# Ending the banks of a GNN aggregate one by one, and moving transposed rows by DMA instead of by TensorE

## The chip, the cores and the metric

The kernel runs on one core of one Trainium2 chip. The metric is the device time of one execution in microseconds (us); lower is better.

## The reference

Two graph layers over 2708 nodes with 1024 features, float32. Each normalises x, forms a score for every pair of nodes, masks it with the adjacency matrix, takes a softmax over the neighbours and adds the weighted mean of the transformed nodes to x.

```python
# layer 0
f = x @ Wf + bf;  g = x @ Wg + bg
scores = where(adj > 0, relu(f @ g.T), NEG)
x_new = softmax(scores, axis=1) @ (x @ W + bW)
# layer 1
h = input @ W
scores = where(adj > 0, leaky_relu(h @ a1 + (h @ a2).T, 0.2), NEG)
x_new = relu(softmax(scores, axis=1) @ h)
# both: h = max(layernorm(x), 0);  x = x + layer(h, adj, ...)
```

## The kernel before

The nodes of the output are cut into five panels of 576, 576, 532, 512 and 512. For each panel and layer there is a *score* stage (layer 0 only), an *aggregate* (softmax weights times features) and a *project* stage (times W). Products use seven half-size products M1 to M7 in place of eight, in the order M1, M5, M2, M6, M3, M7, M4. Each sums in a group of four PSUM banks, and two groups are alive at a time: M6 and M7 (gz) take the banks that M2 (gx) leaves, and what follows M3 takes those that M3 (gy) leaves.

The order of products inside one M, and where its banks are emptied:

```python
            for k, d in ([(k, d) for k in range(K) for d in range(NH)] if by_k else
                         [(k, d) for d in range(NH) for k in range(K)]):
                nc.tensor.matmul(ps[d], left(m, k, d), right(m, k), start=(start and k == 0),
                                 stop=(k == K - 1 and m not in more), skip_group_check=True)
                ...
            if by_k:
                if m in more:
                    more[m](ps)            # the leftover products of all four banks
                for d in range(NH):
                    evict[m](d, ps[d])     # then all four evictions
```

In the middle of M7 the leftover products of M1 and M5 go through four more banks, gw, and VectorE adds them into m15 (the profile calls that tile m):

```python
        def into_m15():
            ps = [bank(f"gw{d}")[:, :h] for d in range(NH)]
            left_over(ps, 1, hi, True)
            for d in range(NH):
                add(get("m15", d), ps[d], get("m15", d))
```

M4's group, gv, takes the banks that gw leaves free. A vector that lies as columns is put on all partitions by TensorE transposes with a broadcast operand:

```python
    def spread(o, cols):
        at = 0
        for g in range(0, len(cols), 4):
            ps = bank("sp_ps")
            ...
                nc.tensor.transpose(ps[:, w:w + n], cl.to_broadcast([n, P]), ident[:n, :n])
            copy(o[:, at:at + w], ps[:, :w])
```

It is used for r (one vector per panel, needed by the score stage as rb) and for two vectors of scores, z and c (the profile calls c "none"), needed by layer 1's weights as ub and vb. While layer 1 aggregates panel p it makes the weights of panel p+1: after M3 the columns (`take_shifts`), after M7 the weights themselves (`take_weights`):

```python
    def take_shifts(p):
        flush()
        got["zm"] = shifts1(p)
    ...
        # one unit of the weights
        nc.scalar.activation(s, vb1[:n, :w], AF.Identity, bias=f2s[:n, t:t + 1])
        nc.vector.scalar_tensor_tensor(s, ub[:n, :w], f[1][:n, t:t + 1], s, op0=OP.add, op1=OP.max)
        add(s, s, mk[0][:n, :w])
        nc.scalar.activation(s, s, AF.Exp)
```

The order of the calls is not the order of the instructions: a scheduler orders each engine's queue at build time, except where the program asks for program order.

## Time and profile before

| | before |
|---|---|
| median, first 3 runs | 3149.56 us (3143.49 to 3149.83) |
| profiled span | 3144.7 us |
| TensorE busy | 3053.0 us, 97% |
| granted TensorE clock, mean | 0.990 |

In the views PE is TensorE (PEld its weight loads), DVE VectorE, ACT ScalarE, POOL GpSimd and SP SyncE; a q behind the name marks the engine's sequencer, which issues DMAs. *Landing* is the time from the issue of a transfer to the semaphore that tells of its end.

The order of time on VectorE and ScalarE around M7 of layer 1's first aggregate (columns: start, length, engine, line, operation, output<-inputs, records, and in brackets the idle time of the engine before it and what ended it):

```profile
2283.87 1.55 DVE L45 TENSOR_TENSOR m<-gw,m 128x288 f32<-128x288 f32 x4 [4.92 <-PE gw L816]
...
2296.14 2.10 ACT L45 ACTIVATE P<-vb,f2s 128x576 f32<-128x576 f32 x3
2296.95 1.55 DVE L45 SCALAR_TENSOR_TENSOR P<-ub,f,P 128x576 f32<-128x576 f32 x2 [2.35 <-ACT P L45]
```

The four adds that empty gw come at 2283.87, 9.3 us ahead of gv's first product at 2293.15. The new weights (P) start 12 us later.

### The profile page before, as it was taken

The page shows a single profiled execution, that of the slowest core. Times are in us where ns is not written, and L with a number is a line of the kernel's source. Part 1 is how long each engine was busy: PE and PEld are TensorE (multiplying, and loading weights), DVE is VectorE, ACT ScalarE, POOL GpSimd, SP SyncE. Part 2 cuts the span into 40 slices and gives each one's busy share as a digit, 9 for nine tenths or more (in the row PEclk, how much of TensorE's full clock was granted, in tenths as well). Part 3 has the DMA queues.
Part 4 walks back from the last instruction along what each step waited for, and adds up shares of the span by engine and source line. Part 5 has one row for each costly group of instructions (what it writes and reads, how often), then busy time and mean ns, then how long its engine had stood idle before and what let it go on. Part 6 is the DMA issues. An engine that isn't in the chain of part 4 may idle for free.

```text
span 3144.7 us, 36222 instructions
## 1 busy us (share of the span) xinstructions
PE 3053.0 (97%) x12712; PEld 2263.8 (72%) x12712; DVE 1827.6 (58%) x3730; ACT 447.0 (14%) x788; POOL 462.8 (15%) x664
## 2 busy tenths in 40 slices
PE   8988999999999999999999999997999999999998
PEld 4566777667877588876888885865757758678684
DVE  5867686286732687327881478658573471745612
ACT  3321020000200102001020002103031130211200
POOL 2643002210002100023000101020010020120102
PEclk9989999999999999999999999998999999999999
DMA  6888938878446796478945677686655565565655
GB/s 215 308 285 270 263 124 310 231 228 252 148 129 168 217 263 200 143 177 245 294 157 153 174 214 235 215 285 209 205 178 174 156 203 156 170 195 172 214 161 192
DMA packets 379045, 651.82 MB, mean 207 GB/s; under 512 B 170784, under 2 KB 211264, under 8 KB 378864
## 3 DMA queue, kind: packets, MB, share of 16 engines
q1 hardware_dynamic: 335920, 525.38, 55.7%
q0 software_dynamic: 42944, 124.13, 11.8%
q8 instruction: 101, 1.65, 0.2%
q14 instruction: 80, 0.66, 0.1%
HBM read 536.68 MB, written 112.67 MB: 206 GB/s over the span
## 4 chain that ended last, share of the span: by engine, by line
PE 83%; DMA 5%; issue 4%; DVE 4%; POOL 2%; SPq 1%; ACT 0%; POOLq 0%; DVEq 0%; ACTq 0%
PE gz L551 12%; PE gy L551 12%; PE gx L551 11%; PE sz L1061 7%; PE gv L551 5%; PE pz L953 5%; PE sy L1061 4%; PE sx L1061 4%; PE px L953 4%; PE py L953 4%; PE qz L551 3%; PE qy L551 2%; PE qx L551 2%; PE M_ps L467 2%; SPq L139 1%
## 5 line engine op out<-in xcount | busy, mean ns | idle before, releaser
L1061 PE MATMUL sz<-B,As 128*128 128x288 f32 (+2 forms) x1200 | 292.7, 393 | 8.2 <-DVE st L45 7.5
L1061 PEld LDWEIGHTS sz<-B,As 128*128 128x128 f32 x1200 | 227.7, 190 | 58.2 <-DVE st L45 11.9
L857 POOL TENSOR_TENSOR gT<-gT,rr 128x2304 f32<-128x2304 f32 (+5 forms) x20 | 72.7, 3635 | 1102.0 <-DVE rr L45 999.3
L1061 PE MATMUL sx<-B,As 128*128 128x288 f32 (+2 forms) x800 | 201.6, 395 | 13.2 <-DMA As<-hs_d 12.2
L1061 PE MATMUL sy<-B,As 128*128 128x288 f32 (+2 forms) x800 | 199.0, 392 | 0.0
L551 PE MATMUL gz<-P,hc 128*128 128x288 f32 (+2 forms) x800 | 186.0, 393 | 2.3 <-ACT gT L45 2.3
L551 PE MATMUL gz<-Sa,hc 128*128 128x288 f32 (+2 forms) x800 | 186.0, 393 | 2.3 <-ACT gT L45 2.3
L551 PE MATMUL gx<-P,hc 128*128 128x288 f32 (+2 forms) x800 | 186.1, 394 | 0.0
L1061 PEld LDWEIGHTS sx<-B,As 128*128 128x128 f32 x800 | 152.3, 191 | 45.4 <-DMA As<-hs_d 13.1
L551 PE MATMUL gy<-T,hc 128*128 128x288 f32 (+2 forms) x800 | 184.2, 391 | 0.0
L551 PEld LDWEIGHTS gz<-Sa,hc 128*128 128x128 f32 x800 | 151.2, 190 | 36.0 <-ACT gT L45 4.4
L551 PEld LDWEIGHTS gx<-P,hc 128*128 128x128 f32 x800 | 153.1, 192 | 32.8 <-issue 1.9
L551 PEld LDWEIGHTS gz<-P,hc 128*128 128x128 f32 x800 | 150.9, 190 | 35.6 <-ACT gT L45 4.4
L551 PEld LDWEIGHTS gy<-T,hc 128*128 128x128 f32 x800 | 152.0, 190 | 30.5
L1061 PEld LDWEIGHTS sy<-B,As 128*128 128x128 f32 x800 | 151.7, 190 | 30.6 <-DVE st L45 0.3
L953 PE MATMUL py<-w,ps 128*128 128x512 f32 x320 | 143.1, 597 | 4.7 <-DMA w<-in_L_gnn_W_dram 4.7
L953 PE MATMUL pz<-w,ps 128*128 128x512 f32 x320 | 142.8, 597 | 0.8 <-DVE pt L45 0.8
L953 PE MATMUL px<-w,gT 128*128 128x512 f32 x320 | 141.9, 596 | 0.7 <-issue 0.7
L143 POOL DMA_DIRECT2D out_dram<-x_res x180 | 88.9, 501 | 265.3 <-DVE x_res L45 259.0
L45 DVE TENSOR_TENSOR gT<-gy,u 128x288 f32<-128x288 f32 (+2 forms) x40 | 14.8, 431 | 183.5 <-PE gy L816 183.5
L953 PEld LDWEIGHTS py<-w,ps 128*128 128x128 f32 x320 | 60.5, 191 | 81.1 <-issue 77.5
L45 DVE TENSOR_TENSOR u<-gz,m 128x288 f32<-128x288 f32 (+2 forms) x40 | 17.6, 439 | 171.1 <-PE gz L551 170.7
(318 smaller groups left out, 5063.6 us busy)
## 6 DMA issues: line engine op xcount, KB each, us to landing
hc<-hg_d SPq DMA_DIRECT2D x350, 512.0 KB, 3.9
As<-hs_d SPq DMA_DIRECT2D x150, 512.0 KB, 5.8
w<-wt_d SPq DMA_DIRECT2D x96, 512.0 KB, 5.1
w<-in_L_gnn_W_dram SPq DMA_DIRECT2D x72, 512.0 KB, 4.3
md<-md_d SPq DMA_DIRECT2D x56, 512.0 KB, 4.6
adj_i<-in_adj_dram SPq DMA_DIRECT2D x200, 128.0 KB, 5.0
hg_d<-g POOLq DMA_DIRECT2D x40, 512.0 KB, 4.9
hs_d<-hsT POOLq DMA_DIRECT2D x40, 512.0 KB, 5.3
```

The source lines that it names most:

```text
L45: i = f(*a, **k)
L139: tc.keep_in_program_order(nc.sync.dma_start(a, b))
L143: nc.gpsimd.dma_start(a, b)
L467: nc.tensor.matmul(ps, wfT[a][c // NH][:, c % NH, :], wgT[b][c], start=(c == 0), stop=(c == NC - 1))
L551: nc.tensor.matmul(ps[d], left(m, k, d), right(m, k), start=(start and k == 0), stop=(k == K - 1 and m not in more), skip_group_check=True)
L857: nc.gpsimd.tensor_tensor(of(e, s), of(e, s), by(s, k), OP.mult)
L953: nc.tensor.matmul(ps, left[i][m][:, k, :], w_[k], start=(start and k == 0), stop=(k == NH - 1), skip_group_check=True)
L1061: nc.tensor.matmul(ps[:n, :h], lefts[q][:, i % 2, c, :n], B[m][c // 2][:, c % 2, :h], start=(start and c == 0), stop=(c == NH - 1), skip_g ...
```

## The change

The intent is threefold: let each bank of an M end on its own, so that its eviction runs beside the next bank's products; take r's spreads off TensorE for panels 1 to 4; and take layer 1's two score spreads off TensorE for panels 1 to 4. Each of these vectors goes to HBM as a row of 4-byte elements and comes back broadcast to all partitions. The cut below leaves out the stop flags and the calls of `behind` (which runs queued softmax work between products); these move with the loops.

```diff
+    def columns_to_row(row, p, col):
+        k = len(pieces[p])
+        nc.gpsimd.dma_start(row[0:1, :W].rearrange("o (i p) -> p (o i)", p=P), col[:, :F])
+        if k > F:
+            n = pieces[p][F][1]
+            nc.gpsimd.dma_start(row[0:1, W:W + n].rearrange("o n -> n o"), col[:n, F:k])
+    def row_on_all(o, row, p):
+        load(o[:, :width[p]], row[0:1, :width[p]].to_broadcast([P, width[p]]))
@@ accumulate
-            for k, d in ([(k, d) for k in range(K) for d in range(NH)] if by_k else
-                         [(k, d) for d in range(NH) for k in range(K)]):
+            whole = K - TAIL                                   # TAIL = 2
+            for k, d in ([(k, d) for k in range(whole) for d in range(NH)] + [(k, d) for d in range(NH) for k in range(whole, K)]
+                         if by_k else [(k, d) for d in range(NH) for k in range(K)]):
...
+                if by_k and d == NH - 1 and k == whole - 1 and m in more:
+                    more[m](ps)
+                if k == K - 1:
                     evict[m](d, ps[d])
...
-                for d in range(NH):
-                    evict[m](d, ps[d])
@@ score stage
-        spread(rb, columns_of(p, r_[:, first_col[p]:]))
+        if p == 0:
+            spread(rb, columns_of(p, r_[:, first_col[p]:]))
+        else:
+            row_on_all(rb, r_d[p], p)
@@ after layer 0's first aggregate
+            for s in range(1, NP):
+                columns_to_row(r_d[s], s, r_[:, first_col[s]:])
@@ weights1
+            if p > 0:
+                for o, row in zip((ub, vb1), uv_d[p]):
+                    row_on_all(o, row, p)
+                return
@@ take_shifts
+        for row, col in zip(uv_d[p], got["zm"]):
+            columns_to_row(row, p, col)
```

More of the change, by code (lines that the diff above doesn't have):

```diff
@@ L162 @@
     mk_d = [dram.tile([P, NQ + 1, 2, width[p]], BF, name=f"mk_d{p}") for p in range(NP)]
+    r_d = [dram.tile([1, WX], FP, name=f"r_d{p}") for p in range(NP)]
+    uv_d = [[dram.tile([1, WX], FP, name=f"uv{k}_d{p}") for k in range(2)] for p in range(NP)]
     x1_d = [dram.tile([P if t < TINY else NY, D], FP, name=f"x1_d{t}") for t in range(NT)]
@@ L535 @@
         picks.append(t)
+    TAIL = 2
     def accumulate(left, right, K, h, order, then, evict, name, prepare={}, rate=0.0, by_k=False, more={}, room=()):
@@ L548, in accumulate @@
             ps = [t[:, :h] for t in acc[at[m]]]
-            for k, d in ([(k, d) for k in range(K) for d in range(NH)] if by_k else
-                         [(k, d) for d in range(NH) for k in range(K)]):
-                nc.tensor.matmul(ps[d], left(m, k, d), right(m, k), start=(start and k == 0),
-                                 stop=(k == K - 1 and m not in more), skip_group_check=True)
-                if by_k and d == NH - 1 and k % 3 == 2:
+            whole = K - TAIL
+            for k, d in ([(k, d) for k in range(whole) for d in range(NH)] + [(k, d) for d in range(NH) for k in range(whole, K)]
+                         if by_k else [(k, d) for d in range(NH) for k in range(K)]):
+                nc.tensor.matmul(ps[d], left(m, k, d), right(m, k), start=(start and k == 0), stop=(k == K - 1),
+                                 skip_group_check=True)
+                if by_k and d == NH - 1 and k < whole and (k % 3 == 2 or k == whole - 1):
                     behind(rate)
@@ L556, in accumulate @@
                     more[m, k]()
-                if not by_k and k == K - 1:
+                if by_k and d == NH - 1 and k == whole - 1 and m in more:
+                    more[m](ps)
+                if k == K - 1:
                     evict[m](d, ps[d])
-                    behind(rate, m in room)
+                    if not by_k:
+                        behind(rate, m in room)
             if by_k:
-                if m in more:
-                    more[m](ps)
-                for d in range(NH):
-                    evict[m](d, ps[d])
                 behind(rate)
@@ L815, in left_over @@
                 g = slice(B32 * d, B32 * d + NY)
-                nc.tensor.matmul(ps[d], two[g, W:], S[TINY][g, s], start=False, stop=True, skip_group_check=True)
+                nc.tensor.matmul(ps[d], two[g, W:], S[TINY][g, s], start=False, stop=start, skip_group_check=True)
         def into_m15():
```

## The prediction

> **What bounds the kernel now.** I read the page first: busy time per engine, the forty slices, the chain that ended last.
>
> ```profile
> span 3144.7 us, 36222 instructions
> PE 3053.0 (97%) x12712; PEld 2263.8 (72%) x12712; DVE 1827.6 (58%) x3730; ACT 447.0 (14%) x788; POOL 462.8 (15%) x664
> PEclk9989999999999999999999999998999999999999
> PE 83%; DMA 5%; issue 4%; DVE 4%; POOL 2%; SPq 1%; ACT 0%; POOLq 0%; DVEq 0%; ACTq 0%
> ```
>
> TensorE is busy 97% of the span at nearly full clock and carries 83% of the chain. So only two things can shorten the program: fewer TensorE cycles, or fewer of the 3144.7 - 3053.0 = 91.7 us in which it stands still. No matrix product goes away, so already here the change is small.
>
> Second, TensorE's waits, totalled by releaser (columns: us in total, times, longest).
>
> ```profile
> PE sx L1061 <- DMA As<-hs_d: 12.2, 2, 12.0
> PE mx_ps L740 <- DVE mx L45: 9.9, 1, 9.9
> PE qx L551 <- ACT m L45: 9.7, 1, 9.7
> PE sum_ps L755 <- DVE gT L45: 5.1, 10, 0.5
> PE gz L551 <- ACT gT L45: 4.5, 10, 0.5
> PE sp_ps L237 <- DVE m L45: 3.0, 1, 3.0
> ```
>
> The change addresses the two rows with count 10, one wait per aggregate (5 panels x 2 layers): M6's banks (gz) wait for M2's eviction to gT, and the row sums (sum_ps) wait for M3's. The long single waits belong to the first panel and the layer boundary; the diff leaves them.
>
> Third, TensorE in order of time at the end of M3 and M7 in layer 1's first aggregate (columns: start, length, line, tiles, records, idle before).
>
> ```profile
> 2264.45 2.10 PE L812 MATMUL gy<-P,hl 128*128 128x288 f32 x8
> 2266.49 0.77 PE L816 MATMUL gy<-P,hl 20*128 20x288 f32 x8
> 2267.79 1.24 PE L755 MATMUL sum_ps<-sm,ones 128*128 128x288 f32 x4 [0.53 <-DVE gT L45]
> ...
> 2283.78 8.03 PE L551 MATMUL gz<-P,hc 128*128 128x288 f32 x32
> 2291.64 0.80 PE L237 MATMUL sp_ps<-ident,z 128*128 128x128 f32 x5
> 2292.37 0.85 PE L237 MATMUL sp_ps<-ident,none 128*128 128x128 f32 x5
> 2293.15 3.18 PE L551 MATMUL gv<-P,hc 128*128 128x288 f32 x12
> ```
>
> The leftover products (hl) end all four banks almost together, then TensorE stands for one eviction. At M7's end, 2293.15 - 2291.64 = 1.51 us go to ten transposes that spread two columns.
>
> **What the Trainium skill says.** (1) "PSUM — Partial Sum Buffer", PSUM bank collisions: engines must not touch one bank and quadrant together, but may use different banks. The trace agrees: the query products, in the same helper but ending bank by bank, show 0.0 us of eviction wait in qz and qy. (2) "DMA: Bandwidth & Descriptors", Rules for kernel authors: a strided last dimension becomes one descriptor per element. The column-to-row write is 512 runs of 4 bytes; this trace has none to HBM. (3) Same page, Anatomy of one DMA: a DMA's semaphore wait is done on the issuing sequencer. The trace agrees: the DMA queue's own waits (SPq) show 281.8 us behind gz alone; its loads issue in program order. (4) "SBUF — State Buffer", Who interferes with whom: a VectorE operation with two SBUF inputs contends with a GpSimd operation that reads SBUF. The trace agrees: an add of 5 elements took 4.60 us beside GpSimd's scaling of 5.04 us.
>
> **The change, part by part.**
>
> *Bank by bank.* The leftover products move ahead of the last two pairs; they cost the same (968.4 to 971.0, about 2.6 us for 288 columns, also where nothing waits, in M7's middle). Then each bank gets its last two pairs alone: 2 products x 2 records x 0.24 us (19.40 us / 80 records) = 0.97 us per bank. The first bank ends 2.9 us before the last; its eviction (0.4 to 0.5 us) is done long before M6 or sum_ps asks for it. M6's fourth bank is asked 1.5 us after M6's start, enough for the last copy. Saving: 4.5 + 5.1 = **9.6 us**. Evictions of M1, M5, M7 and M4 also come earlier, but no wait on TensorE's list is for them: nothing.
>
> *Rows of r.* Four of five spreads leave TensorE (the first panel keeps its own). From the first transpose to the first score product: 0.72, 0.69, 0.44 and 0.48 us, together **2.3 us**. In their place one load per panel of 128 rows of the same 2 KB. Its row was written some 30 us or more earlier, and its load goes ahead of scores' own loads, issued 10 to 20 us before their product: hidden. VectorE loses a copy of 0.68 us per panel, hidden too.
>
> *Layer 1's scores.* Two spreads less at the ends of four aggregates: 1.51, 1.43, 0.87 and 0.87 us, together **4.7 us**.
>
> Sum: 9.6 + 2.3 + 4.7 = 16.6 us, 0.53% of 3149.56.
>
> *What it adds.* The two loads of the score rows stand, in SP's program order, before M4's loads of hc. Today those run far ahead. SP's queue in the same aggregate:
>
> ```profile
> 2241.37 11.96 SPq L139 DMA_DIRECT2D hc<-hg_d  x4
> 2253.38 2.32 SPq L139 DMA_DIRECT2D maskl<-mk_d  x5
> 2256.89 0.32 SPq L139 DMA_DIRECT2D hc<-hg_d  x1
> 2257.30 0.86 SPq L139 DMA_DIRECT2D maskl<-mk_d  x2
> 2260.77 4.20 SPq L139 DMA_DIRECT2D hc<-hg_d  x2
> ```
>
> M4's first hc is among the four from 2241, about 40 us before gv at 2293.15 (the masks after it belong to the next weights, so SP had passed that point). After the change SP must stand there until the rows are in HBM. With E the end of M3 (2267.26): the last column is done at 2278.95, E+11.7 (VectorE behind GpSimd's scaling), some 1 us earlier with the eviction gone: E+10.7. Four small GpSimd DMAs at 0.52 us of issue each (as r<-r of 64 values): E+12.8. Landing: r<-r took 2.9 us, f<-f 5.2, the mask source of 512 runs 5.0; I take 5: E+17.8. Two row loads to issue (0.32 us each), then hc: E+18.5. Landing 3.9 us (median) to 7.0 (a broadcast load, wab): E+22.4 to 25.5. M7 ends at 2291.64 - 0.53, E+23.9. So the new wait is between nothing and 1.6 us, four times: 0 to 6 us, taken as **4 us** because small writes may be slower than I estimate. Panels of 256 and 266 columns have shorter M7 but only two small DMAs: the same margin.
>
> Net: 16.6 - 4 = 12.6 us; 3149.56 - 12.6 = 3137.
>
> **Rivals.** (a) *The row wait takes the place of the spreads.* Speaks for it: 40 us of lead gone, 512 runs of 4 bytes never tried here. At 10 us of landing instead of 5, gv waits about 5 to 6 us four times, some 22 us: about 3155. Against: M7's 22 us almost cover it. (b) *Everything hides*: the rows land in 3 us and hc in 4; then 3133, perhaps 3131 with the two waits of sx for rb's first sum (1.0 us). (c) *VectorE becomes the bound in the tails*, since evictions interleave with the softmax work queued behind them: 58% busy and evictions of 0.4 us against 0.97 us of product per bank speak against; it would give back a few us: about 3142. (d) *The evictions were hidden anyway*: the two rows of waits say no; each wait is in the order of time.
>
> **Range and chances.** Centre 3137; low 3127 (all hidden, plus a faster sample: the runs of before spread over 6 us); high 3150 (most of rival a). Over 2% faster would need 63 us, two thirds of all TensorE idle time: 0.01. Over 2% slower would need 16 us more at each row wait than my worst case: 0.01.
>
> **What the changed profile would show.** The rows "gz <- ACT gT" and "sum_ps <- DVE gT" with 10 waits gone; sp_ps from r on 5 transposes instead of 23, from z and none on 5 each; the first sx right after the last product ahead of it; TensorE busy some 7 us lower; a new wait of gv for hc, or for the rows through SP, of 0 to 2 us four times; DMA packets under 512 B up by some 6,000 (12 columns, 512 each). Wrong would be: gz or sum_ps still waiting (then VectorE or ScalarE's queue held the eviction), gv waiting 5 us or more (rows slow), or sx waiting for rb (its load held back in SP's queue by a buffer not yet free).

## The result, and the profile after

| | before | after |
|---|---|---|
| median of 4 runs | 3148.61 us (3143.49 to 3149.83) | 3173.63 us (3171.73 to 3178.94) |
| profiled span | 3144.7 us | 3170.9 us |
| granted clock, mean | 0.990 | 0.984 |

The ratio is 1.0085, with a 95% interval of 1.0068 to 1.0103. All ratios here are the mean time of one kernel's runs over that of the other's of the same rounds, so not quite the ratio of the medians quoted. The kernel became 25 us slower; that is within 2%, but 24 us above the range predicted.

First the page of the kernel after (span; busy time of the engines; engines in the chain that ended last):

```profile
span 3170.9 us, 36132 instructions
...
PE 3059.0 (96%) x12658; PEld 2272.7 (72%) x12658; DVE 1837.3 (58%) x3721; ACT 447.1 (14%) x779; POOL 475.5 (15%) x682
...
PE 77%; issue 8%; DVE 7%; DMA 5%; POOL 1%; SPq 1%; ACT 0%; DVEq 0%; POOLq 0%; ACTq 0%
```

TensorE does 54 matmuls less (the 54 transposes of r, z and c) and is yet busy 6.0 us longer, and it stands still for 111.9 us where it stood for 91.7. In the chain, VectorE went from 4% to 7%: something waits for it now.

TensorE's waits in the kernel after (total us, times, longest):

```profile
PE gv L567 <- DVE m L45: 17.9, 3, 6.3
...
PE sx L1079 <- DMA As<-hs_d: 7.4, 3, 5.2
...
PE gv L567 <- DMA hc<-hg_d: 6.3, 1, 6.3
...
PE sz L1079 <- DMA As<-hs_d: 5.3, 1, 5.3
```

The two rows of ten waits, gz behind ScalarE and sum_ps behind VectorE, are gone. In their place gv waits four times for 24.2 us together, and the first score stage waits for As in several places, 15.4 us with sy's 2.7, where the kernel before had 12.2, nearly all of it one wait of 12.0.

Where in the span this lies is seen from the stages, each measured from its first to its last product:

| stage | length after minus before, us |
|---|---|
| score, panel 0 | +6.41 |
| layer 0 aggregates, panels 0 to 4 | +1.28, -0.95, -0.90, -0.87, -0.88 |
| project to score, panels 1 to 4 | -0.7, -0.7, -0.4, -0.5 |
| layer 1 aggregates, panels 0 to 3 | +5.71, +5.25, +7.77, +7.24 |
| layer 1 aggregate, panel 4 | -0.88 |

The loss lies in five stages: the four aggregates of layer 1 that prepare a next panel, +25.97 us, and the first score stage. Layer 0's first aggregate may be left aside: three runs of one and the same experiment below had it at -0.39, +1.40 and +1.78, with TensorE's wait for its factors at 3.1, 4.9 and 5.3 us.

Now layer 1's first aggregate in order of time, the same place as the prediction's third view:

```profile
2270.91 1.13 PE L770 MATMUL sum_ps<-sm,ones 128*128 128x288 f32 x4
...
2281.75 0.77 POOL L247 DMA_DIRECT2D uv_d<-z  x1 [1.15 <-DVE none L45]
...
2290.89 0.32 SPq L139 DMA_DIRECT2D ub<-uv_d  x1
2292.45 0.32 SPq L139 DMA_DIRECT2D vb<-uv_d  x1
2292.87 1.08 SPq L139 DMA_DIRECT2D hc<-hg_d  x2
...
2298.72 2.11 ACT L45 ACTIVATE P<-vb,f2s 128x576 f32<-128x576 f32 x3 [17.68 <-DMA vb<-uv_d]
...
2299.53 0.82 DVE L45 SCALAR_TENSOR_TENSOR P<-ub,f,P 128x576 f32<-128x576 f32 x1 [18.00 <-ACT P L45]
...
2300.27 1.54 DVE L45 TENSOR_TENSOR m<-gw,m 128x288 f32<-128x288 f32 x4
...
2300.77 17.25 PE L567 MATMUL gv<-P,hc 128*128 128x288 f32 x64 [5.94 <-DVE m L45]
```

The row sums follow M3 without a wait, as intended. The rows are issued from 2281.75 on. SP can issue the load of ub only at 2290.89 and that of vb at 2292.45, and only then M4's hc. The row vb is on the chip at 2298.7; ScalarE had waited 17.68 us for it, and VectorE 18.00 us for ScalarE. And now see the order: the first P comes *ahead of* the four adds of gw. In the kernel before it came behind them. The adds, whose input had been there for more than 10 us, stand in VectorE's queue behind an instruction that waits for the row. So gw is emptied at 2300.27, and gv's products, which need those banks, wait 5.94 us.

The static order of VectorE's queue confirms that this was decided at build time. Kernel after, first aggregate of layer 1, shortened:

```
z<- ...    none<- ...
P<-ub                                  (needs the row of scores)
m_0<-gw    m_0<-gw    m_1<-gw    m_1<-gw
P<-P,maskl
```

Kernel before: the four m<-gw, then the eight evictions of gz, then P. In three of the four aggregates the first P is ahead of all four adds, in the fourth behind the first of them. It looks as if the scheduler took the rows for ready earlier than the chip has them; its reckoning itself was not looked at.

The transfers of single elements, over the whole span (tile, queue, count, KB, median us from issue to landing):

```profile
r_d<-r POOLq DMA_DIRECT2D x4, 2.0 KB, 10.8
uv_d<-z POOLq DMA_DIRECT2D x4, 2.0 KB, 9.0
```

Hardly any of these 9 us shows as a transfer. In the first aggregate the four writes are issued by 2284.4, and the first of them lands at 2290.6; for 5 us in between the trace has no packet on any of the 16 DMA engines (stretch in us; TensorE's busy time, then records; clock; DMA share, which counts the packets that start in the stretch and so can pass 1; GB/s):

```profile
2285.50:2290.50 5.00, 5.00 (x26) 1.00 0.00 0
```

And the granted clock right after gv's stand, in the same columns:

```profile
2300.77:2306.00 5.23, 5.23 (x16) 0.71 1.06 368
```

The clock granted to TensorE is 0.71 in the 5.2 us after the stand, and 1.00 in the next 12 us. The wait is thus paid a second time. Over the span, gv's products from P take 102.4 us where they took 92.3, a further 10.1 us for the four waits.

With this layer 1 adds up: waits 24.2, slower products 10.1, less four times some 0.9 of the bank part (3.6) and the 4.7 of the spreads, makes 26.0; the stages show 25.97.

The first score stage adds up too: waits for As 15.4 less 12.2, so 3.2, and slower products (sx +0.8, sy +0.9, sz +1.6 by the page's groups) 3.3; together 6.5 against 6.41. The clock is behind these slower products too: in both kernels it was at 0.50 for some 13.6 us of this stage, but before, TensorE worked in only 5.3 us of them (most fell into the one long wait), after in 11.9. The likely reason for the waits, tested below: the scheduler moved the writes of r from the end of layer 0's first aggregate up to between 121 and 290 us, among the stores of hs_d from which As is loaded. Those stores in the window 225 to 315 us, before:

```profile
hs_d<-hsT POOLq DMA_DIRECT2D x12, 512.0 KB, 6.2
```

and after:

```profile
hs_d<-hsT POOLq DMA_DIRECT2D x12, 512.0 KB, 10.6
```

### The profile page after: what moved, and what is told of

It reads as the page before. It is cut to its first block, busy times and chain, and to the rows that moved or that the text cites.

```text
span 3170.9 us, 36132 instructions
## 1 busy us (share of the span) xinstructions
PE 3059.0 (96%) x12658; PEld 2272.7 (72%) x12658; DVE 1837.3 (58%) x3721; ACT 447.1 (14%) x779; POOL 475.5 (15%) x682
## 4 chain that ended last, share of the span: by engine, by line
PE 77%; issue 8%; DVE 7%; DMA 5%; POOL 1%; SPq 1%; ACT 0%; DVEq 0%; POOLq 0%; ACTq 0%
PE gy L567 11%; PE gx L567 11%; PE gz L567 10%; PE gv L567 6%; PE pz L968 6%; PE sz L1079 5%; PE py L968 4%; PE px L968 4%; PE sx L1079 3%; PE sy L1079 3%; PE qz L567 3%; PE qy L567 2%; PE qx L567 2%; DVE junk L45 1%; SPq L139 1%
## 5 line engine op out<-in xcount | busy, mean ns | idle before, releaser
L1079 PEld LDWEIGHTS sz<-B,As 128*128 128x128 f32 x1200 | 229.3, 192 | 63.0 <-DVE st L45 10.8
L567 PE MATMUL gv<-P,hc 128*128 128x288 f32 (+2 forms) x400 | 102.4, 420 | 24.3 <-DVE m L45 17.9
L143 POOL DMA_DIRECT2D mk_d<-mask x55 | 35.9, 653 | 550.7 <-DVE mask L45 543.3
```

Of the source, the lines that this page charges most:

```text
L143: nc.gpsimd.dma_start(a, b)
L1079: nc.tensor.matmul(ps[:n, :h], lefts[q][:, i % 2, c, :n], B[m][c // 2][:, c % 2, :h], start=(start and c == 0), stop=(c == NH - 1), skip_g ...
```

## The experiments

"Before" in the same calls had medians of 3147.26, 3147.84, 3147.32 and 3147.39 us.

### Each part alone: bank_only, r_only, uv_only

Each is the change with the other two parts undone.

```diff
# bank_only: without columns_to_row, r_d, uv_d
# r_only:    accumulate as before; no uv_d
# uv_only:   accumulate as before; no r_d
```

> Only the first part of the change: aggregates end bank by bank; all rows are still spread by TensorE. Theory (the three parts are independent, and in the changed kernel's trace each of the six aggregates without row loads behind them became 0.9 us shorter): ten times 0.95 us, so 9 to 10 us under the kernel before, about 3139 us; the ten waits of gz and the ten of sum_ps are gone. Rival (the evictions only move into VectorE's queue and cost as much there): within 2 us of before.

> Only the second part: the rows of r by DMA for panels 1 to 4. In the changed kernel the scheduler put these small writes among the stores of the first score stage, and that stage was 6.4 us longer. Theory (the 4-byte writes, about 10 us to landing, stand ahead of the hs_d stores[...], and the loads of As wait for those): first score stage 4 to 8 us longer than before, four spreads of 0.44 to 0.72 us gone, in sum 2 to 5 us slower than before, about 3152. Rival (that stage varies by chance from run to run): 2.3 us faster, about 3146, first score stage as before.

> Only the third part: layer 1's score rows by DMA. Theory (the whole loss of layer 1 comes from this part, 6 to 9 us in each of four aggregates, 29.8 us in the changed kernel's trace): about 3178 us, gv waiting 5 to 7 us at four places, layer 0 as before. Rival (the loss needs the new order of the aggregate's end as well, for instance its earlier evictions): about 3146.

| | median, us | ratio to before (95%) |
|---|---|---|
| bank_only | 3138.95 (3134.18 to 3140.51, 5 runs) | 0.9973 (0.9960 to 0.9985) |
| r_only | 3156.65 (3154.22 to 3158.11, 5 runs) | 1.0029 (1.0017 to 1.0042) |
| uv_only | 3176.45 (3174.99 to 3178.08, 4 runs) | 1.0093 (1.0079 to 1.0107) |

Bank by bank gives what was predicted: both rows of ten waits are gone, and the aggregates are 0.88 to 1.03 us shorter, but for layer 0's first with -0.39. The part for r loses 9.4 us, of which the first score stage shows +7.99. The part for layer 1's scores loses 29 us: its four aggregates are +7.43, +5.56, +7.67 and +7.13, the fifth, which has no next panel, 0.00. The sum of the three, -8.3 + 9.4 + 29.2 = +30.3, is near the whole change's +25.0; the intervals of the ratios (some 4 us to each side for a part) do not tell the two apart.

### Is it SP's queue or VectorE's queue? dve_held, hc_ahead, held_and_ahead

Two explanations fit gv's wait: VectorE's queue holds the adds of gw behind P, or SP's queue holds M4's hc behind the row loads. Each can be taken away alone. In dve_held VectorE keeps program order over the stretch in which P was moved up; in hc_ahead M4's first factors are asked for ahead of the rows; held_and_ahead does both.

```diff
# dve_held
     def take_weights(p):
+        if p > 0:
+            nc.hold = ("vector",)
...
         g = aggregate(1, p, S, sm, then, rate=4.0)
+        nc.hold = ()
# hc_ahead
         def scale():
+            if l == 1 and p + 1 < NP:
+                for i in range(0, NQ, 2):
+                    left(M4, i, 0)
```

> The changed kernel, but VectorE's instructions from the end of M7 to the end of M4 in layer 1 keep the program's order, so that the adds from gw and M7's evictions stand ahead of the first softmax operation that needs the rows. Theory (two obstacles side by side, each enough alone: VectorE's queue stands behind a row not yet landed, and M4's hc loads stand behind the row loads in SP's queue): gv no longer waits for VectorE but for hc, 2 to 6 us at four places; 3160 to 3172 us. Rival (VectorE's order alone): no wait of gv, about 3143.

> The changed kernel, but M4's five hc loads are issued ahead of the two row loads. Theory (two obstacles): gv still waits about 6 us for VectorE's adds from gw in each of four aggregates; 3168 to 3175 us. Rival (SP's order alone): no wait of gv, about 3143.

> Both mendings at once. Theory (two obstacles, no third): gv does not wait, layer 1's first four aggregates are 0.95 us (bank by bank) plus 0.9 to 1.5 us (spreads) shorter than before; the first score stage is still about 6 us longer; 3139 to 3145 us. Rival (a third cause, for instance the late softmax itself makes the next aggregate or the projection wait): above 3150.

| | P behind the adds? | hc ahead of rows? | median, us (4 runs each) |
|---|---|---|---|
| after | no | no | 3173.63 |
| dve_held | yes | no | 3175.89 (3168.36 to 3180.56) |
| hc_ahead | no | yes | 3180.59 (3178.84 to 3183.05) |
| held_and_ahead | yes | yes | 3144.13 (3137.46 to 3148.25) |

TensorE's waits for gv, in dve_held:

```profile
PE gv L567 <- DMA hc<-hg_d: 22.6, 4, 6.5
```

and in hc_ahead:

```profile
PE gv L567 <- DVE m L45: 29.8, 4, 7.8
```

Neither single cure helps; both came out above the ranges expected of them. Taking away one obstacle brings out the other at nearly the full size; the releaser in the row changes from VectorE's m to the DMA of hc and back. Taking away both removes the wait: no row for gv is left, and the four aggregates are -2.35, -2.47, -1.78 and -1.75 us against before (as a whole the kernel is at 0.9986 of before, 0.9971 to 1.0001). So there were two obstacles in parallel, each enough by itself. The profile of the change named only the one that ended last, in three of four cases VectorE. What keeps held_and_ahead from the predicted 3137 is the first score stage, +11.91 us in its profile. That stage was 6.4 to 11.9 us longer in all five profiles in which r's rows were written there in 4-byte runs, and within 2 us of before in all others: the part for r.

### Is the landing the root? runs_16b

Both obstacles exist because the rows come late. In this kernel the row takes its elements in another order, such that each partition writes its four elements side by side: 128 runs of 16 bytes in place of 512 of 4, the same 2 KB. Its output is wrong, which doesn't matter for the time.

```diff
-        nc.gpsimd.dma_start(row[0:1, :W].rearrange("o (i p) -> p (o i)", p=P), col[:, :F])
+        nc.gpsimd.dma_start(row[0:1, :W].rearrange("o (p i) -> p (o i)", p=P), col[:, :F])
```

> The changed kernel with one thing altered: each row is written in another order of its elements, so that a partition's four values are one run of 16 bytes (128 runs in place of 512). The result is wrong on purpose. Theory (the landing of about 9 us is the time of 512 four-byte writes): 4 to 6 us to landing, SP goes on some 4 us earlier, gv's wait falls from 6 to 1 or 2 us, and the first score stage is nearer to before; 3145 to 3158 us. Rival (landing does not depend on the number of runs): landing 8 to 9 us, about 3173.

It measured 3136.03 us (3135.74 to 3138.79, 4 runs), ratio 0.9965 (0.9948 to 0.9982). Landing of the first of the two rows:

```profile
uv_d<-z POOLq DMA_DIRECT2D x4, 2.0 KB, 1.7
```

The second took 3.0 us, r's rows 4.3. One wait of gv is left, 2.7 us; the first score stage is at -0.47. One edit of the write's shape takes 37.6 us off the median of the change, more than the theory expected, without a hand in any queue. So the root of both losses is that the rows are written in 4-byte runs.

But the theory's count of runs is not the measure. The tails of 20 or 64 elements were still 4-byte runs here, and the first tail of 64 landed nearly as late as a full row of 512 such runs had:

```profile
uv_d<-z POOLq DMA_DIRECT2D x1, 0.2 KB, 7.0
```

r's two tails, of 64 and 20, took 11.6 and 10.9 us, a later tail of 20 only 1.6. The wait of gv that is left lies in the one aggregate whose next panel has a tail of 64. Why a 4-byte run lands so late is not shown.

### Is r's cost a matter of its place in the queue? bank_r_late

My theory for r was its place: hoisted among the hs_d stores on the same queue, it delays them. Then the same writes pinned to where the program has them, at the end of layer 0's first aggregate, should cost nothing. This is the bank part plus r so pinned.

```diff
-        nc.gpsimd.dma_start(row[0:1, :W]...)
+        tc.keep_in_program_order(nc.gpsimd.dma_start(row[0:1, :W]...))      # both writes of columns_to_row
```

> First and second part, but the writes of r's rows are pinned behind what GpSimd was given before them, so that they run after the first panel's aggregate; no score rows by DMA. Theory (the place of the small writes cost the 6.4 us): 9.5 + 2.3 us under before, about 3137, first score stage as long as before. Rival (it was chance, or it is the traffic itself): no different from bank_only by more than 1 us, or the loss now shows in the stage where the writes run.

It measured 3152.80 us (3149.31 to 3156.55, 5 runs), 14 us over bank_only. The first score stage is normal now (-0.91), but the loss went along with the writes: the project stage of panel 0 became 8.48 us longer, the next score stage 2.49. (Panel 3's score stage is 3.55 us longer too, with TensorE waiting 2.87 us for VectorE's sm where it waited 1.01; that was not followed.) The transfers in the window 590 to 670 us (GB/s in 40 slices of 2 us; then landing):

```profile
GB/s 243 149 33 28 25 15 41 140 10 8 9 128 248 196 199 215 227 177 249 101 322 418 412 388 416 409 399 234 98 75 330 324 297 217 324 173 363 328 18 178
...
x_res<-in_x_dram SPq DMA_DIRECT2D x17, 64.0 KB, 9.4
```

In the kernel before, in the same window:

```profile
x_res<-in_x_dram SPq DMA_DIRECT2D x17, 64.0 KB, 5.0
```

And TensorE in bank_r_late:

```profile
632.17 9.30 PE L967 MATMUL py<-w,ps 128*128 128x512 f32 x16 [6.05 <-DMA w<-wt_d]
```

For 16 us, in two bouts (594 to 604 and 606 to 612 us), no more than 8 to 41 GB/s are moved. The load of x_res is issued by SP, another queue than the writes', and is slowed all the same, from 5.0 to 9.4 us; the factors w come 6.05 us late for TensorE. The theory of the place fell. The cost goes with the writes, wherever they are put: r_d's took 13.5 us here. In the first bout it is not that the DMA engines are busy: from 596 to 604 us the DMA share is 0.30, where the kernel before has 1.12 (from 606 to 612 us it is 0.85 for 1.21). Why 4-byte writes hold up the other queue is not shown by these runs. All were issued from GpSimd's queue; the same writes from another queue were not tried.

### Rows in long runs: turned_plain, turned_ahead, turned_both, bank_again

If the short runs are the fault, make long ones: TensorE transposes the columns once, without broadcast, [128, k] to [k, 128]; ScalarE copies; each row leaves as k runs of 512 bytes. For layer 1 this happens in the middle of M7. turned_ahead also has hc_ahead's edit, turned_both hc_ahead's and dve_held's. These are correct kernels.

```diff
+    def columns_to_rows(cols, to):
+        k = cols[0].shape[1]
+        ps = bank("row_ps", (P, len(cols), P))
+        for i, c in enumerate(cols):
+            nc.tensor.transpose(ps[:k, i, :], c, ident)
+        sb = slot("rows")[:k, :len(cols) * P].rearrange("k (i p) -> k i p", p=P)
+        nc.scalar.copy(sb, ps[:k])
+        for row, i, r0, n in to:
+            nc.gpsimd.dma_start(row[0:1, :n * P].rearrange("o (i p) -> (o i) p", p=P), sb[r0:r0 + n, i, :])
# layer 1: called from into_m15, before left_over; r: once, 18 columns, where the change wrote r_d
```

> A version meant to keep the gains: all three parts, but the columns are first turned by TensorE (one transpose for all of r, two per panel for the score columns, put where M7's middle adds its leftover products), copied by ScalarE, and written to HBM as rows of 512 bytes: 4 or 5 runs where there were 512. VectorE's and SP's orders are left as they come out. Theory (512 short writes were the root; with rows landing 2 to 4 us after issue both queues go on in time): uv rows land in 2 to 4 us, gv waits under 1 us at each place, first score stage as before; 9.5 + 2.2 + 4.0 us under before, about 3132. Rival (any row through HBM comes too late for M4): gv waits 2 to 6 us, 3140 to 3160.

> As turned_plain, with M4's hc loads issued ahead of the row loads. Theory: if the rows are in time, no different from turned_plain (within 2 us), about 3132; if SP's order still cost in turned_plain, faster than it by that wait.

> As turned_ahead, with VectorE's order kept as well. Theory: no wait of gv at all, about 3131 to 3133; at most 2 us from turned_plain. Rival (holding VectorE's order costs the projection, as the 1.9 us in the run with both mendings): slower than turned_ahead by 1 to 3 us.

> The first part alone once more, on the same chip as the turned versions, as their measure. About 9 us under before (3139); the turned versions are 4 to 7 us under it if the rows' gains are real.

| | median, us (5 runs each) | ratio to before (95%) |
|---|---|---|
| turned_plain | 3142.09 (3141.52 to 3143.83) | 0.9985 (0.9972 to 0.9997) |
| turned_ahead | 3139.53 (3137.14 to 3141.08) | 0.9973 (0.9960 to 0.9987) |
| turned_both | 3140.47 (3136.92 to 3145.43) | 0.9980 (0.9967 to 0.9992) |
| bank_again (bank_only once more) | 3137.30 (3134.18 to 3138.09) | 0.9966 (0.9953 to 0.9978) |

In turned_plain, the landing of the rows of five runs:

```profile
uv_d<-rows POOLq DMA_DIRECT2D x4, 2.5 KB, 1.6
```

and gv in the first aggregate, without a wait and at full clock, so 15.68 us where the change had 17.25:

```profile
2291.78 15.68 PE L571 MATMUL gv<-P,hc 128*128 128x288 f32 x64
```

It is not free of waits everywhere: in the fourth aggregate gv waits 2.98 us for hc (the stage is at +1.68), where under 1 us had been expected. turned_ahead, with hc issued earlier, has no wait of gv and is 2.6 us faster by the medians: SP's order still cost something in turned_plain.

The rows land in 1.6 us and layer 1 gains: in turned_ahead the four aggregates are -2.01, -2.25, -1.57 and -1.53. Still all three miss the 3132 us that I had hoped for, and none beats bank by bank alone. Holding VectorE to program order is not needed any more and costs 1.9 us in layer 1's first project stage. The gain of layer 1 is eaten elsewhere: in all three, the first project stage is 1.8 to 2.4 us longer and the second score stage 2.2 to 2.4.

### Does the part for r pay at all? bank_uv_turned, bank_third

Both of those stages lie where r's rows are written and first read. So the last kernel is turned_ahead with r's spreads put back, beside bank_only for the third time.

```diff
# turned_ahead, less:
-            columns_to_rows([r_[:, first_col[1]:]], ...)
-        if p == 0:
-            spread(rb, ...)
-        else:
-            row_on_all(rb, r_d[p], p)
+        spread(rb, columns_of(p, r_[:, first_col[p]:]))
```

> The version with turned rows and M4's first factors loaded ahead, with the part for r taken back to spreads in the four later panels. Theory (each part's worth is the sum of its stages): the bank part gives its 9 to 10 us; the score rows, once in runs of 512 bytes, take a further 1.1 to 1.5 us off each of layer 1's first four aggregates (about 5 us); the part for r, even in long runs, cost some 4 us in the first project stage and the second score stage against the 2.3 us that its spreads save. So this should be at 3133 to 3135 us, 4 us under bank by bank alone, with the first project stage and the second score stage within 0.5 us of the kernel before. Rival: the 4 us there belong to the turned columns' own work or to VectorE's order as it falls with any such change; then they stay without the part for r and the time is 3137 to 3140.

> Bank by bank alone once more, on the same chip and in the same rounds, as the measure for the run beside it: 3137 to 3139 us, 9 to 10 us under the kernel before.

bank_uv_turned measured **3135.75 us** (3133.53 to 3136.64, 5 runs), ratio 0.9964 (0.9952 to 0.9977); bank_third 3140.26 us (3134.67 to 3142.58, 15 runs), ratio 0.9975 (0.9968 to 0.9983). The first project stage and the second score stage are within 0.01 us of before: their loss was the part for r's. Layer 1's four aggregates keep -2.45, -2.24, -1.56 and -1.54. The order of time in the first of them:

```profile
2279.29 1.08 POOL L252 DMA_DIRECT2D uv_d<-rows  x2 [4.54 <-ACT rows L45]
...
2280.96 0.32 SPq L139 DMA_DIRECT2D ub<-uv_d  x1
...
2281.26 1.55 DVE L45 TENSOR_TENSOR m<-gw,m 128x288 f32<-128x288 f32 x4 [5.60 <-PE gw L834]
```

SP passes to ub 1.7 us after the write was issued, where the change needed 9.1, and the adds of gw run at once. This version beats both kernels: it is 11.6 us under before in its own rounds and some 38 us under the change. Against bank by bank alone it is ahead by 4.5 us of medians on the same chip; the two ratios' intervals overlap, and an earlier call had bank by bank at 3137.30, so the medians alone leave 1.6 to 4.5 us. The stages are the firmer evidence: against bank_third in its profile, layer 1's four aggregates are 1.77, 1.30, 0.65 and 0.66 us shorter. What in the part for r costs those 4 us even in long runs was not taken apart; TensorE waits there for VectorE (in turned_plain pt 1.14 and x_res 0.46 us, and st 2.71 where it was 1.01 before).

## Why the prediction was wrong, point by point

The step that failed is *What it adds*: the new wait of gv was put at 0 to 1.6 us, four times, and measured 5.6 to 6.4. Its path through SP and hc was right with one term far too small, the landing; a second path, through VectorE's queue, was missing. The rest of the loss is the lower clock after each of these stands, and r's row, which was called hidden.

- **Bank by bank, 9.6 us: right.** Both rows of ten waits went. Three measurements of this part alone give 8.3, 10.0 and 7.1 us.
- **r's spreads, 2.3 us: right** in size (0.7, 0.7, 0.4, 0.5). **"Hidden" for r's row: wrong.** The step looked only at whether the row would be there in time. It was; but with its writes other transfers landed later (hs_d's stores 10.6 us for 6.2, x_res's loads 9.4 for 5.0), which cost +6.41 us in the change, +7.99 alone, and +8.48 and +2.49 elsewhere when pinned elsewhere.
- **The columns' readiness and the issues: right.** With E the end of M3 (2271.08 after), the last column was due at E+10.7 and came at E+10.5; the four issues due at E+12.8 ended at E+13.3; M7's end, due at E+23.9, was at E+23.75.
- **"I take 5" for the landing: the mis-sized term.** It measured 9.0 us, 10.8 for r. The transfer that gave the 5.0 us, the mask source, has as many runs, but reads longer ones; the 2.9 and 5.2 us were of 64 single elements that stay on the chip; a write of 4-byte elements to HBM had no row in the trace before. I had said so, and still took a figure from transfers of another kind. hc was then issued at E+21.8 instead of E+18.5. With hc's own 3.9 us or more of landing that is at E+25.7 or later, some 2 us or more past M7's end. dve_held, which has this wait alone, measured 22.6 us in four, 5.65 each; there gv's first product came 7.1 us after hc's issue, so hc's landing too was at or above the top of the 3.9 to 7.0 us taken.
- **VectorE's queue: the missing step.** The sum followed the rows to SP and to hc, but not to the engine that uses them. Rival (c) asked only whether softmax work would crowd VectorE. It did not; a single instruction stood at the queue's head for 18 us and held four ready adds behind it. hc_ahead, which has this wait alone, measured 29.8 us in four.
- **Rival (a) had the waits, not the time.** Its time stood outside the prediction's own range, which ended at 3150, and "gv waiting 5 us or more" was named as a sign of being wrong. It put gv's four waits at some 22 us and the time at 3155; they were 24.2 us, the time 3173.63. The difference is what no rival had: the clock after each stand (10.1 us in gv's products, 3.3 in the score stage's) and r's traffic.
- **"TensorE busy some 7 us lower": wrong in sign,** +6.0, for the same reason of the clock: the 54 transposes went, the other products became longer.
- **"DMA packets under 512 B up by some 6,000": wrong.** The count rose by 768, over writes and loads together. It counts packets, not runs (in the trace a full row of 512 runs is 16 packets of 128 bytes), and so does not show the cost.

## What to carry to other kernels

A transfer's size says little when its runs are of one element: turn the data on chip first (two transposes of 0.27 us here) and write long runs, or leave the work on TensorE, where a spread had cost 0.4 to 0.8 us. When a wait is to be moved to a DMA, follow what depends on its landing into *every* in-order queue, the issuing one and those of the consuming engines, and look at what ready work stands behind it; two such waits in parallel hide one another, and undoing only one may show no gain at all. Price each stand of TensorE of several us at more than its length (here 24.2 us of stands cost 10.1 more).

## What the Trainium skill lacked or had wrong

- "DMA: Bandwidth & Descriptors", Specifications and Rules for kernel authors: it says that runs under 512 B are below line rate, that a strided last dimension becomes one descriptor per element, and that a transpose by a plain DMA with a rearranged access pattern differs from the hardware's own by a factor of 19; under "Why small descriptors are slow" it has a fixed overhead per packet. It gives no time for a small write in 4-byte runs. Its fit of about 2.0 us plus bytes over 436 GB/s (section Anatomy of one DMA) would give an estimated 2.0 us for 2 KB. Here 512 runs of 4 bytes to HBM took 9.0 to 13.5 us (medians), 128 runs of 16 bytes 1.7 to 4.3, four or five runs of 512 bytes 1.6 (5.5 for r's rows at a busier time). Nor does the time go with the number of runs: 64 of 4 bytes took 7.0 us and more.
- The same page says that the DMAs of all queues run on the same 16 engines and interleave. No page has that such writes slow the loads of the other queue this far: SP's loads of 64 KB landed in 9.4 us in place of 5.0, and GpSimd's own of 256 KB in 16.6 in place of 5.5, in the same window; in its stretch from 596 to 604 us the DMA share was 0.30 in place of 1.12.
- "TensorE: Matmul & The Clock Gate", What's actually happening: it puts the fall of the clock after an idle window of about 3.4 us. The runs agree in the main: after stands of 5.1 to 7.8 us (after, dve_held, hc_ahead) the clock went to 0.50 each time, after stands of 2.68 and 2.98 us it stayed at 1.00. The 64 products took 17.25 us after a stand of 5.94, 15.79 after one of 2.68, and 15.68 without one. The page prices such waits for a thin matmul kernel that throttles again at each of its 32 tiles, not for single waits in a kernel that is otherwise busy: here four stands of 24.2 us in all cost 10.1 us more.
- No page warns that the scheduler may put an instruction that waits for a DMA ahead of ready work in VectorE's queue; here the head of the queue stood for 18.00 us.
